# A macaron block on one core: the MLP norm's variance by a ones matmul with its power on ScalarE and GpSimd, inputs shifted by DMA, merged weights kept in DRAM, and a new order of steps

## The chip, the cores and the metric

The kernel runs on one core of a Trainium2 chip. The metric is the device time of one execution in microseconds (us); a lower one is better. Everything is computed in fp32 except a mask product in bf16.

## The reference

The input x has 2048 tokens of 128 features. Three parts follow one another, each added to x: half of a transformer, a state-space block (a scan over time with 16 states per channel), and half of the same transformer with the same weights again. Each transformer first takes a layer norm of x and then runs six layers, each with 16 heads of 64, a window of 32 tokens and an MLP of inner width 341:

```python
for i in range(DEPTH):                      # 6
    x = attn_layer(shift_tokens(x), Wqkv[i], q_scale[i], k_scale[i], Wo[i]) + x
    x = ffn_layer(shift_tokens(x), ln_g[i], ln_b[i], W1[i], b1[i], W2[i], b2[i]) + x

def attn_layer(x, Wqkv, qs, ksc, Wo):
    ...
    q = l2norm(q) * qs                      # t / max(norm(t), 1e-12)
    k = l2norm(k) * ksc
    q = q * cos * scale + rotate_half(q) * sin * scale
    k = k * cos * inv + rotate_half(k) * sin * inv
    return local_attention(q, k, v) ... @ Wo    # each token sees its window and the one before

def ffn_layer(x, g, bln, W1, b1, W2, b2):
    mu = x.mean(-1, keepdims=True)
    var = ((x - mu) ** 2).mean(-1, keepdims=True)
    xn = (x - mu) / jnp.sqrt(var + 1e-05) * g + bln
    a, gate = jnp.split(xn @ W1 + b1, 2, -1)
    return a * jax.nn.gelu(gate, approximate=False) @ W2 + b2
```

`shift_tokens` takes the upper 64 features from the token before.

## The kernel before, in words

Activations stay in SBUF with features on partitions: `r0` feeds the attention, `r1` the MLP, each 2048 columns and a pad of 32; the writers store the upper 64 features one column further on, which is the token shift (`halves`). A tile is 128 tokens, 16 to a layer and 96 to a transformer; a block is four tiles (512 tokens). The attention works on tiles, the MLP on blocks.

The engines run in the order in which `run` issues (a manual schedule for PE, DVE, ACT and POOL; SP, which issues the loads, is left to the framework). `run` goes through iterations i; in each it goes down the list `ORDER` of pairs (step, lag) and issues the step for tile i - lag, so that up to eight tiles are under way. An MLP step runs only for the last tile of a block, in every fourth iteration. A layer's loads, biases and merge are issued at fixed iterations ahead of the list.

The steps of a tile, by the tables `TILE` and `BLOCK`: PQ and PK project queries and keys into PSUM (L252, `x_ps`); SQ and SK square them on ACT (L264); T1 and T2 multiply by cosines and sines on DVE (L270, L276); AQ and AK add the two on POOL (L285); UQ and UK sum the squares on DVE (L291, `ss`). The norm of queries and keys takes a floor at 1e-24 on DVE (NM, `floors`, L298), exp(-0.5 ln) on ACT (NL, `roots`, L303 and L304) and a Newton step of three small DVE products (NN, `norms`, L309, L310, L312). CQ and CK multiply by it on POOL (L316). RQ and RK transpose on PE (L329, `t_ps`), EQ and EK copy out on ACT (L338, L343), EP copies the previous window's keys (L350). S makes the scores: two masks in bf16 (L366) and 64 small products (L377, `s_ps`). MX takes maxima on DVE (L393), ES copies out on ACT (L388), SB subtracts on POOL (L399), EX exponentiates on ACT (L405), SM sums and inverts on DVE (L410, L411), DV divides on POOL (L415), TP transposes on DVE (L425).

The values aren't projected: XT transposes the inputs of the tile on PE, once for its own 128 tokens and once for those 32 earlier (`inputs`, L434, `i_ps`), EXW copies both out in one go (`inputs_out`, L441, `xw`), and PX averages inputs by the attention weights (L450, `z_ps`, 16 instructions on 32-row groups). EZ0 and EZ1 copy that out (L462, `zt`), ZM mixes with 16 matrices of 128x128 that are Wv times Wo per head (L470, `y_ps`), and RS adds the residual (L480). These merged matrices `w.m` are made by `merge` from Wv and Wo, for each layer in each transformer (PE L201, copies on ACT L208).

The steps of a block: F1 centres by a matmul (L492), XC and SF copy and square on ACT (L503, L508). V sums the squares of each token by four matmuls against a column of 1/128 (L88, `v_ps`), so that the variances lie on partitions; VE adds the epsilon on DVE (L518); PW raises to the power -0.5 on POOL and puts it on a diagonal (L108, L110); RB spreads it over partitions by a matmul of ones (L120, `rb_ps`); XN multiplies centred values, gain and spread on DVE (L533). G and A are the two halves of the first MLP product (L543), GL the gelu on ACT with a table load before and after (L562, L670), H the product (L574), Y the second product (L587) and YR the residual (L598).

Large PSUM tiles (`bank2`, two banks) rotate over three buffers, small ones (`bank`) over two. So a product waits until the third `bank2` before it has been read.

## Time and profile before

| | |
|---|---|
| median of 3 runs | 3683.08 us (3682.62 to 3688.38) |
| the profiled execution: its time, its span | 3705.84 us, 3704.0 us |
| granted TensorE clock, mean | 0.957 |
| busy share of the span: PE, DVE, POOL, ACT | 94%, 88%, 71%, 59% |
| mixing products of tiles, first and last: first transformer | 103.6 and 1597.1 us from the start |
| the same, second transformer | 2173.5 and 3668.5 us |
| DMA | 66.50 MB, 18 GB/s on average |

The span is the time from the first to the last instruction in the trace; the run's own time is 1.84 us longer. Busy shares are averages over the two transformers and the state-space block between them (about 1626 to 2095 us), in which DVE works and PE partly waits. A row of a timeline or of the chain of waits gives the start, the duration, the engine, the line, what is written from what and how many instructions are merged. A matmul's duration reaches past the start of the next one, since they are pipelined; the difference of two starts is the time that one took in a full queue. In rows of groups the numbers after the bar are the busy time in us, the mean of one in ns and the idle time ahead of them with what ended it. fp32 products count as two instructions each, transposes as one.

### The profile page before, as it was taken

The page shows a single profiled execution, that of the slowest core. Times are in us where ns is not written, and L with a number is a line of the kernel's source. Part 1 is how long each engine was busy: PE and PEld are TensorE (multiplying, and loading weights), DVE is VectorE, ACT ScalarE, POOL GpSimd, SP SyncE. Part 2 cuts the span into 40 slices and gives each one's busy share as a digit, 9 for nine tenths or more (in the row PEclk, how much of TensorE's full clock was granted, in tenths as well). Part 3 has the DMA queues.
Part 4 walks back from the last instruction along what each step waited for, and adds up shares of the span by engine and source line. Part 5 has one row for each costly group of instructions (what it writes and reads, how often), then busy time and mean ns, then how long its engine had stood idle before and what let it go on. Part 6 is the DMA issues. An engine that isn't in the chain of part 4 may idle for free.

```text
span 3704.0 us, 94599 instructions
## 1 busy us (share of the span) xinstructions
PE 3494.9 (94%) x41968; PEld 2239.0 (60%) x41968; DVE 3259.9 (88%) x3954; ACT 2168.4 (59%) x2884; POOL 2621.3 (71%) x1450
## 2 busy tenths in 40 slices
PE   6999999999999999976999789999999999999997
PEld 3666666666666666642222356666666666666664
DVE  4989999999999999847889778999999999999994
ACT  2666666666666666634222277666666666666664
POOL 4878878888888888721100188888888888888883
PEclk7999999999999999986779899999999999999998
DMA  2000010000000000000000200000001000000000
GB/s 92 13 19 25 13 36 11 26 19 19 19 19 19 8 13 7 2 7 0 1 0 0 68 7 25 19 19 19 25 13 36 8 19 30 13 13 7 14 2 13
DMA packets 45504, 66.50 MB, mean 18 GB/s; under 512 B 2412, under 2 KB 35496, under 8 KB 43560
## 3 DMA queue, kind: packets, MB, share of 16 engines
q1 hardware_dynamic: 45096, 60.45, 5.3%
q8 instruction: 331, 5.42, 0.6%
q14 instruction: 77, 0.63, 0.1%
HBM read 59.39 MB, written 1.05 MB: 16 GB/s over the span
## 4 chain that ended last, share of the span: by engine, by line
PE 27%; DVE 19%; issue 5%; ACT 4%; POOL 1%; DMA 0%; POOLq 0%; DVEq 0%; ACTq 0%
PE y_ps L470 5%; PE x_ps L252 5%; DVE rot L270 3%; DVE ss L291 3%; PE z_ps L450 3%; DVE st L843 2%; PE t_ps L329 2%; PE y L850 2%; PE s_ps L377 2%; DVE t L276 2%; PE a_ps L543 2%; DVE ss L298 2%; PE o_ps L587 2%; DVE rs L410 1%; DVE mx L393 1%
## 5 line engine op out<-in xcount | busy, mean ns | idle before, releaser
L285 POOL TENSOR_TENSOR rot<-rot,t 128x1024 f32<-128x1024 f32 x384 | 900.0, 2364 | 89.2 <-DVE rot L270 86.1
L316 POOL TENSOR_TENSOR rot<-rot,rn 128x1024 f32<-128x1024 f32 x384 | 722.5, 1902 | 135.4 <-DVE rn L312 135.4
L470 PEld LDWEIGHTS y_ps<-zt,m 128*128 128x128 f32 x6144 | 717.5, 192 | 99.6 <-issue 81.9
L470 PE MATMUL y_ps<-zt,m 128*128 128x128 f32 x6144 | 719.0, 275 | 6.3 <-ACT zt L462 6.3
L252 PE MATMUL x_ps<-qk,r 128*128 128x512 f32 x1536 | 703.6, 600 | 10.5 <-ACT zt L462 8.5
L264 ACT ACTIVATE sq<-x_ps 128x1024 f32<-128x1024 f32 x384 | 389.1, 1025 | 447.0 <-DVE t L276 446.3
L415 POOL TENSOR_TENSOR pr<-pr,rs 128x1024 f32<-128x1024 f32 x192 | 364.9, 1900 | 254.9 <-DVE rs L411 253.6
L276 DVE TENSOR_TENSOR t<-x_ps,tab 128x1024 f32<-128x1024 f32 x384 | 461.6, 1203 | 66.1 <-PE x_ps L252 65.7
L252 PEld LDWEIGHTS x_ps<-qk,r 128*128 128x128 f32 x1536 | 285.7, 191 | 356.2 <-issue 313.2
L270 DVE TENSOR_TENSOR rot<-x_ps,tab 128x1024 f32<-128x1024 f32 x384 | 467.3, 1218 | 37.1 <-ACT sq L264 31.3
L291 DVE TENSOR_REDUCE ss<-sq 128x16 f32<-128x1024 f32 x384 | 448.8, 1210 | 1.4
L329 PE MATMUL t_ps<-cs,rot 128*128 128x128 f32 x3072 | 388.7, 278 | 47.0 <-POOL rot L316 46.9
L450 PE MATMUL z_ps<-pt,xw 32*128 32x512 f32 x3072 | 387.9, 614 | 17.0 <-DVE rot L270 13.0
L462 ACT COPY zt<-z_ps 128x1024 f32<-128x1024 f32 x384 | 388.6, 1013 | 25.3 <-PE z_ps L450 21.9
L329 PEld LDWEIGHTS t_ps<-cs,rot 128*128 128x128 f32 x3072 | 352.8, 144 | 80.6 <-POOL rot L316 57.1
L343 ACT COPY kt<-t_ps 128x1024 f32<-128x1024 f32 x192 | 194.6, 1014 | 320.9 <-PE t_ps L329 320.9
L399 POOL TENSOR_TENSOR pr<-pr,mx 128x1024 f32<-128x1024 f32 x192 | 365.3, 1903 | 1.2 <-ACT pr L388 1.2
L377 PEld LDWEIGHTS s_ps<-kt,qt 64*32 64x32 f32 x24576 | 255.3, 105 | 115.7 <-issue 60.7
L377 PE MATMUL s_ps<-kt,qt 64*32 64x64 f32 x24576 | 290.1, 225 | 11.6 <-issue 9.0
L388 ACT COPY pr<-s_ps 128x1024 f32<-128x1024 f32 x192 | 194.5, 1013 | 170.3 <-DVE mx L393 170.3
L298 DVE SCALAR_TENSOR_TENSOR ss<-ss 128x32 f32<-128x32 f32 x192 | 258.1, 1344 | 6.5
L837 ACT ACTIVATE da<-delta,a_neg 128x512 f32<-128x512 f32 x128 | 92.2, 722 | 252.2 <-DVE st L843 247.5
(133 smaller groups left out, 4980.0 us busy)
## 6 DMA issues: line engine op xcount, KB each, us to landing
tab<-in_tabs_dram SPq DMA_DIRECT2D x48, 512.0 KB, 3.5
qk<-in_wqk_dram SPq DMA_DIRECT2D x12, 1024.0 KB, 5.4
wv<-in_wv_dram SPq DMA_DIRECT2D x12, 512.0 KB, 4.2
wo<-in_wo_dram SPq DMA_DIRECT2D x12, 512.0 KB
w<-in_w_dram SPq DMA_DIRECT2D x12, 341.0 KB, 7.4
w<-in_w_dram SPq DMA_DIRECT2D x12, 128.0 KB, 2.1
xi<-in_x_dram SPq DMA_DIRECT2D x4, 256.0 KB
out_dram<-xo SPq DMA_DIRECT2D x4, 256.0 KB
```

The costliest lines, as they stand in the source:

```text
L252: nc.tensor.matmul(out=x[:, j], lhsT=self.r0[:, bass.ds(PAD + g % NT * P, P)], rhs=self.w[g // NT].qk[:, bass.ds(kind * INNER + j * 512, 5 ...
L264: self.nc.scalar.activation(st.sq[kind], st.x[kind], AF.Square)
L270: self.nc.vector.tensor_tensor(st.rot[kind], st.x[kind], cos, ALU.mult)
L276: self.nc.vector.tensor_tensor(st.t2[kind].rearrange("p h (two c) -> p h two c", two=2), st.x[kind].rearrange("p h (two c) -> p h two c", ...
L285: self.nc.gpsimd.tensor_tensor(st.rot[kind], st.rot[kind], st.t2[kind], ALU.add)
L291: self.nc.vector.tensor_reduce(st.ss[:, kind, :], st.sq[kind], AX.X, ALU.add)
L316: self.nc.gpsimd.tensor_tensor(st.rot[kind], st.rot[kind], st.rn[:, kind, :].unsqueeze(2).to_broadcast([P, HEADS, DH]), ALU.mult,)
L329: self.nc.tensor.transpose(t_ps[:, c, :], flat[:, bass.ts(c, P)], self.k.ident)
L377: nc.tensor.matmul(out=st.s[32 * b : 32 * b + 32, par, c, :], lhsT=st.qt[rows, c, bass.ts(b, WIN)], rhs=st.kt[rows, c, bass.ds(WIN * b, 2 ...
L450: self.nc.tensor.matmul(out=st.z[b // 2][:, b % 2].rearrange("p (h q) -> p h q", q=WIN), lhsT=st.xw[rows, j, :], rhs=st.pt[rows, :, j, :], ...
L462: self.nc.scalar.copy(st.zt[:, 2 * half : 2 * half + 2].rearrange("p b h q -> p b (h q)"), st.z[half])
L470: self.nc.tensor.matmul(out=st.y_ps.rearrange("p (b q) -> p b q", q=WIN), lhsT=self.w[g // NT].m[:, h // 2, h % 2, :], rhs=st.zt[:, :, h, ...
```

## The change

In the MLP norm V is one matmul of a 128x128 matrix of ones with the squares, which gives the sum of each token on all partitions. VE (three ACT instructions of 128x512) makes variance plus epsilon and exp(-0.5 ln) of it; XN (five POOL instructions of 128x512) does a Newton step and multiplies by the centred values. PW and RB are gone. The gain goes into W1, which ACT scales once per layer after `biases` has read it. In the norm of queries and keys the floor is a Relu of (ss - 1e-24) on ACT with 1e-24 added again later, and the first of the three DVE products is a Square on ACT. XT transposes the tile's own 128 tokens only; EXW copies them and two DMAs that ACT issues build the half that lies 32 tokens earlier, from this tile (96 partitions) and the one before (32 partitions), with three buffers. In the first transformer SP stores each layer's merged matrices to DRAM after `merge`; in the second it loads them instead of Wv and Wo, and nothing is merged. `ORDER` is new: RQ, RK, EQ, EK, EP, S and MX go from lag 1 to 2, SB, EX and SM from 2 to 3, XT and EXW from 1 to 3, PX, EZ0 and EZ1 from 3 to 4, ZM, RS and F1 from 4 to 5, XN from 5 to 6, A from 6 to 7, UQ and NL from 0 to 1, AQ from 0 to 1; PK stands first among PE's steps of an iteration, PQ stands between PX and S.

```diff
-    ("DV", 3), ("ES", 2), ("XC", 5), ("G", 6), ("NN", 1), ("PK", 0), ("SF", 5), ("CQ", 1),
-    ("GL", 6), ("H", 7), ("PQ", 0), ("CK", 1), ("T2K", 0), ("SK", 0), ("TP", 3), ("T2Q", 0),
-    ("ZM", 4), ("T1K", 0), ("SB", 2), ("Y", 7), ("SQ", 0), ("RK", 1), ("V", 5), ("EK", 1),
-    ("RS", 4), ("T1Q", 0), ("YR", 7), ("VE", 5), ("RQ", 1), ("EQ", 1), ("EP", 1), ("UK", 0),
-    ("PW", 5), ("XT", 1), ("PX", 3), ("RB", 5), ("UQ", 0), ("S", 1), ("F1", 4), ("AK", 0),
-    ("NM", 0), ("EX", 2), ("EZ0", 3), ("AQ", 0), ("XN", 5), ("NL", 0), ("EXW", 1), ("TB", 7),
-    ("EZ1", 3), ("A", 6), ("SM", 2), ("MX", 1),
+    ("SB", 3), ("GL", 7), ("PK", 0), ("AQ", 1), ("T1K", 0), ("SK", 0), ("ZM", 5), ("UQ", 1),
+    ("RS", 5), ("T2K", 0), ("A", 7), ("EX", 3), ("XN", 6), ("RK", 2), ("H", 7), ("RQ", 2),
+    ("EK", 2), ("SM", 3), ("UK", 0), ("EQ", 2), ("NL", 1), ("F1", 5), ("XT", 3), ("NN", 1),
+    ("PX", 4), ("PQ", 0), ("AK", 0), ("EP", 2), ("DV", 3), ("EZ0", 4), ("CQ", 1), ("CK", 1),
+    ("XC", 5), ("S", 2), ("EXW", 3), ("SF", 5), ("EZ1", 4), ("T2Q", 0), ("V", 5), ("ES", 2),
+    ("TB", 3), ("T1Q", 0), ("G", 6), ("Y", 7), ("SQ", 0), ("MX", 2), ("VE", 5), ("TP", 3),
+    ("YR", 7),
...
+        if self.again:
+            w.m = wp.tile([P, 8, 2, P], F32, tag="m", name="m")
+            nc.sync.dma_start(out=w.m.rearrange("p c j f -> p (c j f)"), in_=k.merged[layer])
+            return
...
     def merge(self, layer):
+        if self.again:
+            return
...
+        nc.sync.dma_start(
+            out=self.k.merged[layer], in_=w.m.rearrange("p c j f -> p (c j f)")
+        )
     def biases(self, layer):
...
+        nc.scalar.activation(w.w1, w.w1, AF.Identity, scale=self.vec(V_G + layer))
...
-    def floors(self, g):
-        s = self.at[g].ss
-        self.nc.vector.scalar_tensor_tensor(s, s, 1e-24, s, ALU.max, ALU.max)
     def roots(self, g):
-        st = self.at[g]
+        nc, k, st = self.nc, self.k, self.at[g]
+        nc.scalar.activation(st.ss, st.ss, AF.Relu, bias=k.minus_tiny)
         st.y = self.sb.tile([P, 2, HEADS], F32, tag="y0", name="y0")
-        self.nc.scalar.activation(st.y, st.ss, AF.Ln)
-        self.nc.scalar.activation(st.y, st.y, AF.Exp, scale=-0.5)
+        nc.scalar.activation(st.y, st.ss, AF.Ln, bias=k.tiny)
+        nc.scalar.activation(st.y, st.y, AF.Exp, scale=-0.5)
+        st.y2 = self.sb.tile([P, 2, HEADS], F32, tag="y2", name="y2")
+        nc.scalar.activation(st.y2, st.y, AF.Square, scale=float(np.sqrt(0.5)))
     def norms(self, g):
...
-        nc.vector.scalar_tensor_tensor(y2, st.y, -0.5, st.y, ALU.mult, ALU.mult)
-        nc.vector.scalar_tensor_tensor(y2, y2, 1.0, st.ss, ALU.mult, ALU.mult)
+        nc.vector.scalar_tensor_tensor(st.y2, st.ss, 1e-24, st.y2, ALU.add, ALU.mult)
...
-        nc.vector.scalar_tensor_tensor(st.rn, y2, 1.5, st.y, ALU.add, ALU.mult)
+        nc.vector.scalar_tensor_tensor(st.rn, st.y2, 1.5, st.y, ALU.subtract, ALU.mult)
     def inputs(self, g):
-        st.i_ps = self.bank("i_ps")[:, 0:256].rearrange("p (j f) -> p j f", f=P)
-        for j in range(2):
-            self.nc.tensor.transpose(
-                st.i_ps[:, j, :], self.r0[:, bass.ds(g % NT * P + WIN * j, P)], self.k.ident
-            )
+        st.i_ps = self.bank("i_ps")[:, 0:P]
+        self.nc.tensor.transpose(
+            st.i_ps, self.r0[:, bass.ds(PAD + g % NT * P, P)], self.k.ident
+        )
     def inputs_out(self, g):
-        self.nc.scalar.copy(st.xw, st.i_ps)
+        st.xw = self.sb.tile([P, 2, P], F32, tag="xw", name="xw", bufs=3)
+        nc.scalar.copy(st.xw[:, 1], st.i_ps)
+        nc.scalar.dma_start(out=st.xw[WIN:, 0], in_=st.xw[0 : P - WIN, 1])
+        if g % NT:
+            nc.scalar.dma_start(out=st.xw[0:WIN, 0], in_=self.at[g - 1].xw[P - WIN :, 1])
+        else:
+            nc.gpsimd.memset(st.xw[0:WIN, 0], 0.0)
     def variance(self, f):
-        variances(self.k, ff.sq, ff.v_ps)
+        self.nc.tensor.matmul(out=ff.v_ps, lhsT=self.k.ones, rhs=ff.sq, start=True, stop=True)
     def variance_out(self, f):
-        self.nc.vector.tensor_scalar(ff.ve, ff.v_ps[:, 0:4], LN_EPS, None, ALU.add)
-    def deviation(self, f):
...
-    def spread(self, f):
...
+        ff.ve = sb.tile([P, 512], F32, tag="ve2", name="ve", bufs=1)
+        nc.scalar.activation(ff.ve, ff.v_ps, AF.Identity, bias=k.eps, scale=1.0 / P)
+        ff.rs = sb.tile([P, 512], F32, tag="fsq", name="rs", bufs=1)
+        nc.scalar.activation(ff.rs, ff.ve, AF.Ln)
+        nc.scalar.activation(ff.rs, ff.rs, AF.Exp, scale=-0.5)
     def normal(self, f):
-        nc.vector.scalar_tensor_tensor(
-            ff.xn, ff.xc, self.vec(V_G + layer), ff.rb, ALU.mult, ALU.mult
-        )
+        nc.gpsimd.tensor_tensor(t, ff.rs, ff.rs, ALU.mult)
+        nc.gpsimd.tensor_tensor(t, t, ff.ve, ALU.mult)
+        nc.gpsimd.tensor_scalar(t, t, -0.5, 1.5, ALU.mult, ALU.add)
+        nc.gpsimd.tensor_tensor(t, t, ff.rs, ALU.mult)
+        nc.gpsimd.tensor_tensor(t, ff.xc, t, ALU.mult)
...
-    transformer(k, xt)
+    transformer(k, xt, False)
     state_space(k, xt)
-    transformer(k, xt)
+    transformer(k, xt, True)
```

## The prediction

> **What bounds the kernel now.** I read the busy shares first, then the spacing of one operation over whole layers, then the order of TensorE's work inside one tile. The busy shares:
>
> ```profile
> PE 3494.9 (94%) x41968; PEld 2239.0 (60%) x41968; DVE 3259.9 (88%) x3954; ACT 2168.4 (59%) x2884; POOL 2621.3 (71%) x1450
> ```
>
> Two stretches of about four tiles in the middle of a transformer, from the table by stretches (length, then busy PE, PEld, DVE, ACT, POOL, the clock, the DMA share):
>
> ```profile
> 800.00:863.10 63.10, 62.26 (x849) 42.40 (x848) 58.90 (x74) 40.57 (x54) 52.72 (x29) 1.00 0.03 10
> 863.10:927.00 63.90, 63.51 (x852) 42.99 (x851) 60.66 (x73) 41.16 (x56) 53.99 (x28) 1.00 0.06 18
> ```
>
> PE is busy 125.8 of 127.0 us at full clock, DVE 119.6, POOL 106.7, ACT 81.7. Busy PE can hide stalls, so I take start-to-start times. In the chain of waits the mixing product (L470) of tiles 16 apart, in the second transformer:
>
> ```profile
> 2203.60 3.57 PE y_ps L470 x32
> ...
> 2457.96 3.57 PE y_ps L470 x32
> ```
>
> A layer is 254.4 us (the next two spacings are 254.5 and 254.4). Now the timeline of PE, with a block's norm in the first tile and none in the second:
>
> ```profile
> 866.16 3.73 PE L470 MATMUL y_ps<-zt,m 128*128 128x128 f32 x32
> 869.73 1.04 PE L329 MATMUL t_ps<-cs,rot 128*128 128x128 f32 x8
> 870.60 0.95 PE L88 MATMUL v_ps<-inv,sq 128*128 128x1 f32 x8
> 871.41 1.07 PE L329 MATMUL t_ps<-cs,rot 128*128 128x128 f32 x8
> 872.33 0.38 PE L434 MATMUL i_ps<-cs,r 128*128 128x128 f32 x2
> 872.64 2.00 PE L450 MATMUL z_ps<-pt,xw 32*128 32x512 f32 x16
> 874.57 1.13 PE L120 MATMUL rb_ps<-dg,ones 128*128 128x512 f32 x2
> 875.62 0.39 PE L366 MATMUL s_ps<-masks 32*128 32x512 bf16 x2
> 875.94 1.48 PE L377 MATMUL s_ps<-kt,qt 64*32 64x64 f32 x128
> 877.35 2.84 PE L543 MATMUL g_ps<-xn,w 128*128 128x512 f32 x6
> 880.03 3.60 PE L252 MATMUL x_ps<-qk,r 128*128 128x512 f32 x8
> ...
> 889.27 2.00 PE L450 MATMUL z_ps<-pt,xw 32*128 32x512 f32 x16
> 891.06 0.42 PE L366 MATMUL s_ps<-masks 32*128 32x512 bf16 x2
> 891.41 1.48 PE L377 MATMUL s_ps<-kt,qt 64*32 64x64 f32 x128
> ```
>
> Differences of starts give the price of each group: x 3.43, y 3.57, t 1.74, i 0.45 (0.31 to 0.49), z 1.79, masks 0.35, s 1.41: 12.74 a tile, 203.8 in sixteen. A block adds c 0.97, v 0.86 (0.81, and 0.05 because it splits t), rb 1.16 (872.64 to 875.94 is 3.30; without rb 889.27 to 891.41 is 2.14), g 2.68, a 2.68, o 2.58: 10.93, 43.7 in four blocks. The merge is 2.2 (733.56 to 735.84 in its timeline), the biases 1.4 (17.3 us over 12 layers in the groups). Together 251.1 of 254.4: PE's own work bounds the kernel, with 3.3 us of stall in a layer, 40 in all.
>
> **What the Trainium skill says.** "SBUF — State Buffer", section "SBUF: two separate sides": a VectorE instruction with two SBUF inputs and a GpSimd instruction take a shared port pair exclusively; the later one waits for the whole instruction. The trace agrees: the tiny product L298 takes 1.34 us on average, 0.23 in one tile and 1.78 in another, while L310, of the same shape, takes 0.20. "GPSIMD Engine Reference", section 3.1: a two-input fp32 operation costs GpSimd 1.96 times VectorE's time; here 2.36 us (L285) against 1.20 (L276), 1.97 times. "TensorE: Matmul & The Clock Gate", section "The mechanism" of Part 3: weights load ahead of running matmuls only if row groups differ; the 0.30 us that rb costs above its own 0.86 (two matmuls at x's 0.43) agrees with a lost overlap at a change between row-tiled and full-array work, but shows the price only. "DMA: Bandwidth & Descriptors", section "Anatomy of one DMA": a fixed time of some 2 us, mostly completion; this trace's smallest loads land in 2.1 us.
>
> **The change on PE, the path that sets the end.** (1) One input transpose less a tile: t gives 1.74/16 = 0.11 each; bounds 0.11 to 0.22, taken 0.11, 1.8 a layer. (2) v and rb go, 4 x (0.86 + 1.16) = 8.1; one ones matmul of 128x512 comes, 4 x 0.86 = 3.4. (3) The new order splits x: keys' half ahead of the mixing, queries' half between z and the masks. That puts a full-array matmul between row-tiled ones in every tile: 16 x 0.30 = 4.8 a layer. Bounds 0 (another wait covers the reloading) and 0.45 (half as much again); taken 0.30, since rb stood in the very same place. Sum: 1.6 less a layer, 19 in 12 layers. (4) The second transformer doesn't merge: 6 x 2.2 = 13.
>
> **Off PE, per four tiles of 63.5 us.** DVE loses the floors (L298), one of three steps of the norm, the normalizing product and the epsilon, with these groups of 800 to 1200 us:
>
> ```profile
> L298 DVE SCALAR_TENSOR_TENSOR ss<-ss 128x32 f32<-128x32 f32 x25 | 35.4, 1414 | 0.9
> L309 DVE SCALAR_TENSOR_TENSOR y<-y 128x32 f32<-128x32 f32 x26 | 27.3, 1051 | 0.0
> L415 POOL TENSOR_TENSOR pr<-pr,rs 128x1024 f32<-128x1024 f32 x26 | 49.4, 1901 | 30.7 <-DVE rs L411 30.7
> ```
>
> 4 x 1.41 + 4 x 0.19 + 0.74 + 0.15 = 7.3 of 59.8. The port wait of L309 (1.05 against 0.19) I leave on the new first product, which also has two SBUF inputs; bounds 0.19 and 1.41. DVE isn't the bound, so this is worth only what of PE's 40 us of stall comes from it. POOL loses the power and the diagonal, 1.02 + 1.04, and gains five operations of 128x512. The diagonal at 1.04 and its like at 1024 columns, 1.90, give 0.18 fixed; a product of full operands is then 0.18 + (2.36 - 0.18)/2 = 1.27, four 5.1; the one-input step is bounded by 0.6 (half) and 1.27, taken 0.8: 5.9 together. POOL goes from 53.4 to 57.2. ACT gains two 128x32 activations a tile (0.23 each), three of 128x512 a block (0.63) and two DMA issues a tile, 0.33 to 0.58 in SP's timeline, taken 0.4; the copy falls from 0.35 to about 0.24: 40.9 becomes 47.5. What hides it all is PE's 62. Were the cover gone, each would cost its full size. The issue waits on ACT for the copy ahead of it; behind it queue a block's squares (SF), the second copy of z (EZ1), the scores' copy (ES) and the squares of q (SQ), and PE waits for EZ1 with its next keys' projection. The shifted half lands some 2 to 3 us after issue and is read one iteration later, over 8 us on. POOL's XN, 5.9 in one go, stands ahead of AK, DV, CQ and CK; PE wants the keys' turn 5.3 us into the next iteration (x half 1.7, y 3.6), which is what POOL may be late.
>
> SP is passed too: in the first transformer a store of 1 MB follows each merge and waits on SP for ACT's copies (1.0 each), with the next loads of Wo and of a table behind it, both used iterations later; in the second one load of 1 MB replaces two of 0.5. At a DMA share of 0.03 to 0.06 nothing waits for these. Scaling W1 on ACT (12 times some 0.8) comes several iterations before its use.
>
> The stalls: PE's weight loads for the scores wait 40.1 us in the whole run for ACT (pr L405) and those of x 30.2 (zt L462), ACT in turn for DVE; with longer lags and 7.3 us less DVE half of the 40 should go, bounds none and all: -20. The ends: the last block's chain has nothing beside it. v at the cold clock takes 2.1 instead of 1.05; three ACT steps (1.9) and POOL's 5.9 replace 0.16, 1.01, 1.04, rb 2.07 and xn 0.75: 9.9 against 6.1, +4 an end, +7 for both.
>
> Sum: -19 - 13 - 20 + 7 = -45. It is made against the profiled execution (span 3704.0, run 3705.84), which lies 0.6% over the median of 3683.08; I take the difference off the median: 3638.
>
> **Rivals.** *A, the forecast*: 3638, own range 3612 to 3665. *B, reloading hidden, stalls gone*: the 4.8 a layer falls away and all 40 us go: -58 - 20 more, 3560; half of that, 3600, is likelier. For: the turns of queries and keys and the averaging each stand one iteration later behind their inputs, which leaves slack. Against: rb paid the price in that place. *C, new waits eat the gain*: PE's stalls grow by 3.3 a layer instead of halving, +60 on A, say 3680: for it speak ACT's longer queue ahead of EZ1 and the burst on POOL. *D, slower: POOL's queue becomes the bound.* Its idle time is 10.1 of 63.5 in four tiles, about half of it ahead of L415, waiting for DVE's divisors. POOL's work will be 57.2; if all its waits stay, its cycle is 67.3, 3.8 over today, x 48 blocks = +182: 3865. It decides from 6.3 of the 10.1 us on. Against: DVE, whom it waits for, gets lighter, and the divisors stand early in the new order.
>
> **Numbers.** A 0.50, B 0.22, C 0.15, D 0.13. The measurement can't tell less than 0.2%, 7.4 us, from no change. Faster: A, B and half of C, 0.79; same 0.08 from C; slower D, 0.13. The range is 3575 to 3692: below it lies the end of B, 0.05, above it D, 0.13.
>
> **What would show it.** The 16-tile spacing of y should be near 251 in the first transformer and 249 in the second; z to masks should take 2.2 more than 1.79 (x half 1.72, switch 0.30 and its share); L298 gone, the first product of the norm still near 1 us; the five POOL steps near 5.9. If z to masks shows no price, B holds. If POOL is busy over 95% in the middle and PE waits for POOL's rot, D. If PE waits for ACT zt, C.

## The result and the profile after

| | before | after |
|---|---|---|
| median | 3689.49 us (20 runs, 3677.99 to 3712.70) | 3686.01 us (20 runs, 3664.97 to 3698.81) |
| ratio to before, 95% interval | | 0.9979 (0.9962 to 0.9996) |
| span of the profiled execution | 3704.0 us | 3693.0 us |

The forecast was 3638 from 3683, 45 us less. Measured are 0.2% less, 7.7 us with an interval of 1 to 14 (the two medians lie 3.5 apart): the sign is right, five sixths of the gain are missing. The busy times on the page of the kernel after:

```profile
PE 3483.3 (94%) x41200; PEld 2167.3 (59%) x41200; DVE 3020.2 (82%) x3477; ACT 2338.7 (63%) x3414; POOL 2784.8 (75%) x1606
```

DVE has lost 240 us and PE 12; ACT and POOL have gained 170 and 164. None of that says where the time went, so I cut both spans at the same landmarks, the starts of the mixing products `y_ps` and of the projections `x_ps`. The third column is the first experiment, explained below.

| stage, us | before | after | after, one table load more |
|---|---|---|---|
| start to first mixing product | 103.6 | 102.1 | 105.9 |
| first transformer, first to last mixing product | 1493.5 | 1479.2 | 1478.5 |
| from there, through the state-space block, to the second transformer's first projection | 517.7 | 524.6 | 515.3 |
| first projection to first mixing product | 58.7 | 68.1 | 60.6 |
| second transformer, first to last mixing product | 1495.0 | 1480.0 | 1462.2 |
| last mixing product to end | 35.6 | 39.1 | 38.7 |

The stage with the state-space block takes 491 to 527 us over the fourteen profiled executions, and its length follows the clock granted to PE there: 491 to 494 us at a mean of 0.83 to 0.84 in six of them, 509 to 527 at 0.76 to 0.79 in the other eight. Between the kernel with two transposes below (492.0) and the kernel after (524.6) PE's busy time in this stage is 395 and 437 us, while DVE is busy for 392 and 394 and ACT for 152 in both. That fits the spread of 14 to 47 us between the runs of one kernel, which goes with their mean granted clock, but only one execution of each kernel was profiled. It is why I read stages beside totals.

Two things stand out. The first transformer gains 14.3 us where 20 were forecast. The second gains 15 where 33 were, and loses 9.4 on the way to its first mixing product. Where in the second? Its mixing products 16 tiles apart, from the chain of waits of the kernel after:

```profile
2174.14 3.57 PE y_ps L485 x32
...
2434.67 3.59 PE y_ps L485 x32
...
2685.67 3.59 PE y_ps L485 x32
```

The first sixteen take 260.5, the next 251.0 (before: 250.8 and 254.2). So its layers do run faster, and the loss sits at its head. In the middle (layers two to five of each transformer, y to y) a layer falls from 254.5 to 253.3 in the first transformer and from 254.4 to 250.7 in the second; the prediction expected near 251 and 249. The middle, in the timeline of PE, with a block's norm in the first tile:

```profile
847.15 1.02 PE L507 MATMUL c_ps<-r,cs 128*128 128x512 f32 x2
848.01 0.27 PE L442 MATMUL i_ps<-cs,r 128*128 128x128 f32 x1
848.21 2.00 PE L465 MATMUL z_ps<-pt,xw 32*128 32x512 f32 x16
850.14 1.98 PE L263 MATMUL x_ps<-qk,r 128*128 128x512 f32 x4
852.06 0.39 PE L376 MATMUL s_ps<-masks 32*128 32x512 bf16 x2
852.38 1.56 PE L387 MATMUL s_ps<-kt,qt 64*32 64x64 f32 x128
853.87 1.12 PE L529 MATMUL v_ps<-sq,ones 128*128 128x512 f32 x2
854.83 1.90 PE L263 MATMUL x_ps<-qk,r 128*128 128x512 f32 x4
856.57 3.73 PE L485 MATMUL y_ps<-zt,m 128*128 128x128 f32 x32
...
866.43 1.55 PE L387 MATMUL s_ps<-kt,qt 64*32 64x64 f32 x128
868.09 2.81 PE L556 MATMUL g_ps<-xn,w 128*128 128x512 f32 x6
```

Read it by differences of starts. The variance is one group of 0.96 in place of v and rb (0.81 and 1.06 on average). The queries' half between z and the masks takes 1.92, the keys' half further down 1.74; z takes 1.93 where it took 1.79: the price of changing over that step (3) foresaw. And the scores, 1.41 before, take 1.49 ahead of v and 1.66 ahead of g. That last number is a wait; whose, the second experiment tells. The groups of 800 to 1200 us, busy time and mean ns after the bar:

```profile
L322 DVE SCALAR_TENSOR_TENSOR rn<-y,y 128x32 f32<-128x32 f32 x26 | 26.5, 1018 | 0.9
L320 DVE SCALAR_TENSOR_TENSOR y<-ss,y 128x32 f32<-128x32 f32 x26 | 15.3, 588 | 1.4 <-ACT y L316 1.4
L548 POOL TENSOR_TENSOR xn<-xc,xn 128x512 f32<-128x512 f32 x7 | 9.2, 1311 | 0.5
L545 POOL TENSOR_TENSOR xn<-xn,ve 128x512 f32<-128x512 f32 x7 | 8.9, 1274 | 0.6
...
L544 POOL TENSOR_TENSOR xn<-rs 128x512 f32<-128x512 f32 x6 | 6.3, 1046 | 0.0
...
L546 POOL TENSOR_SCALAR xn<-xn 128x512 f32<-128x512 f32 x7 | 4.3, 619 | 0.6
```

POOL's five steps, L544 to L548, sum to 5.5 (5.9 forecast). The floor L298 is gone, but the last product of the norm, L322, with operands of the same kinds and sizes, took 0.19 before as L312:

```profile
L312 DVE SCALAR_TENSOR_TENSOR rn<-y,y 128x32 f32<-128x32 f32 x26 | 5.0, 192 | 0.9
```

Now it takes 1.02. The wait for POOL that the prediction described for L298 has moved on to it: between 180 and 1540 us 48 of its 86 instructions are long (1.8 us in the median), and each of these began while a POOL instruction ran and ended with it (0.05 us later in the median); the other 38 take 0.19. No run here tests the wait by itself.

### The profile page after: what moved, and what is told of

Its sections match the earlier page's. It is cut to its first block, busy times and chain, and to the rows that moved or that the text cites. A ratio compares the mean times of both kernels' runs of the same rounds, so it can differ in the third digit from the quotient of the medians.

```text
span 3693.0 us, 93340 instructions
## 1 busy us (share of the span) xinstructions
PE 3483.3 (94%) x41200; PEld 2167.3 (59%) x41200; DVE 3020.2 (82%) x3477; ACT 2338.7 (63%) x3414; POOL 2784.8 (75%) x1606
## 4 chain that ended last, share of the span: by engine, by line
PE 78%; DVE 10%; issue 5%; ACT 4%; POOL 2%; ACTq 1%; DMA 0%; POOLq 0%; SPq 0%; DVEq 0%
PE x_ps L263 18%; PE y_ps L485 17%; PE z_ps L465 10%; PE s_ps L387 7%; PE t_ps L339 4%; PE g_ps L556 4%; PE a_ps L556 3%; PE o_ps L600 3%; DVE t L287 3%; PE y L863 3%; DVE st L856 2%; PE s_ps L376 2%; PE c_ps L845 1%; DVE r L495 1%; PE b_ps L845 1%
## 5 line engine op out<-in xcount | busy, mean ns | idle before, releaser
L263 PE MATMUL x_ps<-qk,r 128*128 128x512 f32 x1536 | 758.6, 617 | 10.3 <-ACT sq L275 5.1
L287 DVE TENSOR_TENSOR t<-x_ps,tab 128x1024 f32<-128x1024 f32 x384 | 469.3, 1222 | 82.9 <-PE x_ps L263 73.9
L263 PEld LDWEIGHTS x_ps<-qk,r 128*128 128x128 f32 x1536 | 271.7, 192 | 421.4 <-issue 226.4
L465 PE MATMUL z_ps<-pt,xw 32*128 32x512 f32 x3072 | 400.8, 614 | 13.1 <-DVE t L287 5.2
L339 PE MATMUL t_ps<-cs,rot 128*128 128x128 f32 x3072 | 370.1, 274 | 19.7 <-POOL rot L326 19.7
L425 POOL TENSOR_TENSOR pr<-pr,rs 128x1024 f32<-128x1024 f32 x192 | 365.2, 1902 | 21.3 <-DVE rs L421 13.4
L403 DVE TENSOR_REDUCE mx<-s_ps 128x16 f32<-128x1024 f32 x192 | 235.0, 1224 | 127.1 <-ACT pr L398 125.4
L387 PE MATMUL s_ps<-kt,qt 64*32 64x64 f32 x24576 | 298.5, 227 | 7.0 <-ACT kt L360 7.0
L387 PEld LDWEIGHTS s_ps<-kt,qt 64*32 64x32 f32 x24576 | 267.0, 105 | 55.0 <-issue 45.9
L435 DVE STREAM_TRANSPOSE pt<-pr 128x1024 f32<-128x1024 f32 x192 | 237.4, 1237 | 43.0 <-POOL pr L425 43.0
L850 ACT ACTIVATE da<-delta,a_neg 128x512 f32<-128x512 f32 x128 | 92.2, 722 | 260.3 <-DVE st L856 255.6
```

The source lines that it names most:

```text
L263: nc.tensor.matmul(out=x[:, j], lhsT=self.r0[:, bass.ds(PAD + g % NT * P, P)], rhs=self.w[g // NT].qk[:, bass.ds(kind * INNER + j * 512, 5 ...
L287: self.nc.vector.tensor_tensor(st.t2[kind].rearrange("p h (two c) -> p h two c", two=2), st.x[kind].rearrange("p h (two c) -> p h two c", ...
L339: self.nc.tensor.transpose(t_ps[:, c, :], flat[:, bass.ts(c, P)], self.k.ident)
L387: nc.tensor.matmul(out=st.s[32 * b : 32 * b + 32, par, c, :], lhsT=st.qt[rows, c, bass.ts(b, WIN)], rhs=st.kt[rows, c, bass.ds(WIN * b, 2 ...
L465: self.nc.tensor.matmul(out=st.z[b // 2][:, b % 2].rearrange("p (h q) -> p h q", q=WIN), lhsT=st.xw[rows, j, :], rhs=st.pt[rows, :, j, :], ...
```

## Experiments

My theory after the traces: the middle gains what PE's own sum says, and the queue of ACT, made longer by the change, takes it back in two places: at the second transformer's head, where loads of activation tables (the function tables that ACT needs before a logarithm or an exponential) lie uncovered, and behind the two DMA issues of every tile. The rival: the new order itself is at fault, with its switch between z and the masks, and another order would keep the gain. Each ratio below is to the kernel before, measured beside it on the same chip; the medians of two different experiments were not taken side by side.

### The table loads at the second transformer's head

In the kernel after ACT loads tables twice in each of nine tiles there. Its timeline, with its DMA issues (ACTq):

```profile
2164.61 0.34 ACT L311 ACTIVATE ss<-ss,minus_tiny 128x32 f32<-128x32 f32 x1
2164.97 1.28 ACT L313 ACT_TABLE_LOAD   x1
2166.26 0.32 ACT L313 ACTIVATE y<-ss,tiny 128x32 f32<-128x32 f32 x1
2166.60 1.28 ACT L314 ACT_TABLE_LOAD   x1
2167.89 0.23 ACT L314 ACTIVATE y<-y 128x32 f32<-128x32 f32 x1
2168.16 0.23 ACT L316 ACTIVATE y<-y 128x32 f32<-128x32 f32 x1
2168.29 0.49 ACT L360 ACTIVATE kt<-kt,cs 128x256 f32<-128x256 f32 x1
2168.69 0.99 ACT L477 COPY zt<-z_ps 128x1024 f32<-128x1024 f32 x1
```

and PE in the same moment:

```profile
2169.73 0.39 PE L376 MATMUL s_ps<-masks 32*128 32x512 bf16 x2 [1.97 <-ACT zt L477]
```

The logarithm and the exponential each get a table of their own until the first gelu's load at L683 sets the one that holds both; the explicit load at the head of `run` doesn't appear in the trace of this transformer. The Trainium skill, "ScalarE: Activation LUTs", section "Table sets: the hidden batching unit", gives a logarithm followed by an exponential one load, since one set has both; here a tile shows two. "ScalarE activation tables: per-element evaluation and per-set limits", section "Table sets in the compiler and the runtime", says that the compiler places the loads per block of the program, which fits but is not tested here. The kernel before has the same nine pairs (L303 and L304); the kernel after has two loads more, for its first block's norm (L536 and L537). One explicit load, in the first iteration of each transformer:

```diff
                     getattr(self, method)(g, *args)
+                    if i == 0 and name == "SK":
+                        activation_tables(self.nc, EXP_LN)
```

> The changed kernel with the activation table of exp and ln loaded once at the start of the second transformer, so that the two loads per tile in its first nine tiles (and two for its first block) go. Theory 1 (the gain of the middle was given back at the ends, above all here, where ACT's queue has become longer): the first 16 tiles of the second transformer take 249 to 252 us instead of 260.5, the span 9 to 15 us less than the 3693 of the changed kernel. Theory 2 (the new order's price on PE and new stalls in the middle eat the gain): the head isn't the cause, 0 to 4 us.

Measured: 3664.04 (3639.56 to 3678.17), ratio 0.9898 (0.9848 to 0.9948). The first 16 tiles take 243.9 instead of 260.5, the way to the first mixing product 60.6 instead of 68.1. Of the stages in the table above, 17.8 and 7.5 are gone, 25 us together; the stretch to the first mixing product, which lasts 102 to 107 us over all the profiles, takes 3.8 more.

The same line in the kernel before:

> The kernel before with the same single table load, after the first iteration's last step. Theory 1 (the nine reloaded tables cost only where ACT's queue in the second transformer's head is on the path, which the new queue made it): before's own nine pairs lay beside other work, so at most 3 us of the whole are won, 3690 to 3698 beside before's 3698, and first x to first y of the second transformer stays at 57 to 59 us, its first 16 tiles at 248 to 251. Rival (the loads cost their 2.6 us a tile whatever the queue): 20 us faster as in the new kernel.

Measured: 3699.88, ratio 0.9994 (0.9968 to 1.0021); the head falls from 58.7 to 55.5 and the first 16 tiles from 250.8 to 247.9. So the same loads cost the kernel before 6 us by stages, which is less than its ratio can tell, and the kernel after 25. There too they held up a copy that PE waits for, the second of z:

```profile
2171.70 1.98 PE L252 MATMUL x_ps<-qk,r 128*128 128x512 f32 x4 [1.83 <-ACT zt L462]
```

Apart from two of the twenty loads, then, the change didn't add the loads but their place: now they stand ahead of the copies of the previous window's keys and of both halves of z.

### The shifted inputs: one transpose and two DMAs, or two transposes

On top of the table load, the old `inputs` and `inputs_out`, with two buffers for `xw` as before (not all lines are shown):

```diff
...
+        for j in range(2):
+            self.nc.tensor.transpose(
+                st.i_ps[:, j, :], self.r0[:, bass.ds(g % NT * P + WIN * j, P)], self.k.ident
+            )
...
-        nc.scalar.copy(st.xw[:, 1], st.i_ps)
-        nc.scalar.dma_start(out=st.xw[WIN:, 0], in_=st.xw[0 : P - WIN, 1])
...
-            nc.scalar.dma_start(out=st.xw[0:WIN, 0], in_=self.at[g - 1].xw[P - WIN :, 1])
...
+        self.nc.scalar.copy(st.xw, st.i_ps)
```

> The new kernel with the table load, but with the old inputs: two input transposes and one copy of 128x256 instead of one transpose, a copy of 128x128 and two DMAs issued by ACT. Beside the new kernel with the table load (3664 in its own call). The prediction's step (1): PE does 0.11 to 0.16 us more in each of 192 tiles, 21 to 31 us slower. Rival (ACT's two issues, 1.1 us a tile, are what keeps PE's stalls from falling): slower by less than 10 us or faster.

Measured: 3617.85 (3612.74 to 3643.80), ratio 0.9785 (0.9741 to 0.9830): faster, the opposite of what my step (1) says, and the fastest kernel of this study. Layers take 251.7 instead of 253.1 and 248.5 instead of 250.4; the two transformers lose 12.3 and 11.3 us between their first and last mixing products, 24 in all, and the way to the second's first mixing product is 2.2 longer (62.8 against 60.6), so that 22 remain. The profile of this run has the state-space stage at 492.0, 23 us under that of the run with the table load alone; the clock granted there (0.84 against 0.78) explains this part. Runs of one kernel differ by as much, so the ratio may flatter the change. The lowest times of the two kernels differ by 27. I take 22 to 27 as the effect.

Where it comes from shows in ACT's timeline, in the kernel after:

```profile
864.54 0.99 ACT L477 COPY zt<-z_ps 128x1024 f32<-128x1024 f32 x1
865.43 0.27 ACT L451 COPY xw<-i_ps 128x128 f32<-128x128 f32 x1
865.73 0.52 ACTq L452 DMA_DIRECT2D xw<-xw  x1
866.28 0.61 ACTq L454 DMA_DIRECT2D xw<-xw  x1
866.93 1.01 ACT L477 COPY zt<-z_ps 128x1024 f32<-128x1024 f32 x1 [1.24 <-PE x_ps L263]
```

and with two transposes:

```profile
862.33 0.99 ACT L472 COPY zt<-z_ps 128x1024 f32<-128x1024 f32 x1
863.23 0.37 ACT L451 COPY xw<-i_ps 128x256 f32<-128x256 f32 x1
863.49 1.02 ACT L472 COPY zt<-z_ps 128x1024 f32<-128x1024 f32 x1
```

The second copy of z ends at 867.94 in the first: PE has finished its scores by about 867.8 (1.41 after 866.43) and starts g only at 868.09, behind the copy. With two transposes it ends at 864.51, the scores run from 864.23, and g starts 1.41 later, without a wait. (The label "PE x_ps" on the idle 1.24 misleads, as labels can: the two issues fill it.) In the middle of the first transformer the scores' start to the next start is 1.53 on average with the DMAs and 1.42 without, 0.12 in each tile, 1.9 a layer (2.3 in the second transformer); the second transpose costs PE 0.06 (0.28 to 0.34 at L442 and L444), 0.9 a layer.

Is it ACT's time or the DMA? The same two DMAs from SP's queue:

```diff
-        nc.scalar.dma_start(out=st.xw[WIN:, 0], in_=st.xw[0 : P - WIN, 1])
+        nc.sync.dma_start(out=st.xw[WIN:, 0], in_=st.xw[0 : P - WIN, 1])
...
-            nc.scalar.dma_start(out=st.xw[0:WIN, 0], in_=self.at[g - 1].xw[P - WIN :, 1])
+            nc.sync.dma_start(out=st.xw[0:WIN, 0], in_=self.at[g - 1].xw[P - WIN :, 1])
```

> The new kernel with the table load, the two shifting DMAs of a tile issued by SP's queue instead of ACT's. If ACT's issue time (two issues, 0.55 to 0.6 us each and a wait ahead of each) is what delays the squares and copies behind them: the 16-tile spacing of the middle falls as with two transposes, to 251.5 to 252 in the first and 248.5 to 249 in the second transformer, 20 to 25 us less in all than the new kernel with the table load. If it is the DMA itself or the wait for the copy: the spacing stays at 253.1 and 250.5.

Measured: 3639.26 (3621.41 to 3642.06), ratio 0.9826 (0.9791 to 0.9861). The transformers lose 9.3 and 9.4 us between their mixing products, 19 of the 24; a layer takes 252.4 and 249.1, a little over what I expected. The Trainium skill, "DMA: Bandwidth & Descriptors", section "Issuing engines are not separate DMA queues", says that another issuing engine saves no more than the sequencer's time to initiate a DMA; that is all that is saved here, and it is worth 19 us. So most of the cost is ACT's time for the issues, shown; the rest is small, and even with SP the DMAs are not ahead of a second transpose.

And the two transposes alone, without the table load:

> The new kernel without the added table load, with the old inputs (two transposes and one copy). If the two causes are separate (table loads in the head of the second transformer about 25 us, ACT's DMA issues 24 to 27 us in the middle), it lies about 26 us under the new kernel, middle at 251.7 and 248.5 a layer, and its second transformer's first 16 tiles still near 260, near 3659. If the issues are also part of what uncovers the loads in the head, the first 16 tiles fall towards 245 and the whole towards 3640.

Measured: 3663.99 (3633.20 to 3666.60), ratio 0.9895 (0.9850 to 0.9941), 22 below the kernel after by medians; the stages other than the state-space block give 29. Layers again 251.7 and 248.5, the first 16 tiles of the second transformer at 255.6, between my two numbers: the shorter queue covers some of the table loads, 18 us of them stay (13.4 there, 4.8 ahead of it, against the run with both).

### The order, and the switch between z and the masks

Scores ahead of the queries' half, in the kernel after:

```diff
-    ("PX", 4), ("PQ", 0), ("AK", 0), ("EP", 2), ("DV", 3), ("EZ0", 4), ("CQ", 1), ("CK", 1),
-    ("XC", 5), ("S", 2), ("EXW", 3), ("SF", 5), ("EZ1", 4), ("T2Q", 0), ("V", 5), ("ES", 2),
-    ("TB", 3), ("T1Q", 0), ("G", 6), ("Y", 7), ("SQ", 0), ("MX", 2), ("VE", 5), ("TP", 3),
+    ("PX", 4), ("AK", 0), ("EP", 2), ("DV", 3), ("EZ0", 4), ("CQ", 1), ("CK", 1),
+    ("XC", 5), ("S", 2), ("PQ", 0), ("EXW", 3), ("SF", 5), ("EZ1", 4), ("MX", 2), ("T2Q", 0), ("V", 5), ("ES", 2),
+    ("TB", 3), ("T1Q", 0), ("G", 6), ("Y", 7), ("SQ", 0), ("VE", 5), ("TP", 3),
```

> The changed kernel with the scores (S) ahead of the queries' projection (PQ), so that all row-tiled groups of PE stand together again; MX goes ahead of T2Q. Theory 2: the price of the split vanishes, z back to 1.79, x to 1.72 to 1.75 each; 0.39 us a tile, 6.3 a layer, some 60 to 75 us in all, span 3620 to 3635. Rival: the rotation of the PSUM buffers turns it into waits of the same size (the scores need the buffer that EQ reads), span 3670 to 3710. Theory 1 alone expects no more than 10 us either way.

Measured: 3724.81, ratio 1.0072 (1.0048 to 1.0095). In this kernel's timeline of PE:

```profile
875.69 2.02 PE L465 MATMUL z_ps<-pt,xw 32*128 32x512 f32 x16
877.51 0.41 PE L376 MATMUL s_ps<-masks 32*128 32x512 bf16 x2
878.13 1.48 PE L387 MATMUL s_ps<-kt,qt 64*32 64x64 f32 x128 [0.21 <-ACT kt L360]
```

z to masks is 1.82: without the switch z is as cheap as before, and the scores after the masks take their 1.41. But the masks take 0.62, since the scores now wait for ACT's copy of the keys before (L360), and layers are 255 to 258 in the first transformer. The masks are the smaller part of it, 3.8 us a layer. The two halves of the projection lose more, 4.6 a layer although the switch is gone, where PE waits behind them for ACT, as ahead of g:

```profile
879.73 1.86 ACTq L454 DMA_DIRECT2D xw<-xw  x1
881.62 1.01 ACT L477 COPY zt<-z_ps 128x1024 f32<-128x1024 f32 x1 [2.48 <-PE x_ps L263]
882.78 2.81 PE L556 MATMUL g_ps<-xn,w 128*128 128x512 f32 x6 [1.26 <-ACT zt L477]
```

That copy stands behind the DMA issues, of which the second takes 1.86 here. This order was not run with two transposes, which would take just these issues away. So I tried to give ACT what it needs sooner, EP ahead of EQ and the norm's roots after the first copy of z, with the table load:

```diff
-    ("EK", 2), ("SM", 3), ("UK", 0), ("EQ", 2), ("NL", 1), ("F1", 5), ("XT", 3), ("NN", 1),
-    ("PX", 4), ("PQ", 0), ("AK", 0), ("EP", 2), ("DV", 3), ("EZ0", 4), ("CQ", 1), ("CK", 1),
-    ("XC", 5), ("S", 2), ("EXW", 3), ("SF", 5), ("EZ1", 4), ("T2Q", 0), ("V", 5), ("ES", 2),
-    ("TB", 3), ("T1Q", 0), ("G", 6), ("Y", 7), ("SQ", 0), ("MX", 2), ("VE", 5), ("TP", 3),
+    ("EK", 2), ("EP", 2), ("SM", 3), ("UK", 0), ("EQ", 2), ("F1", 5), ("XT", 3), ("PX", 4),
+    ("AK", 0), ("DV", 3), ("EZ0", 4), ("NL", 1), ("NN", 1), ("CQ", 1), ("CK", 1),
+    ("XC", 5), ("S", 2), ("PQ", 0), ("EXW", 3), ("SF", 5), ("EZ1", 4), ("MX", 2), ("ES", 2),
+    ("T2Q", 0), ("V", 5), ("TB", 3), ("T1Q", 0), ("G", 6), ("Y", 7), ("SQ", 0), ("VE", 5), ("TP", 3),
```

> The new kernel with the table load and another order: the masks and scores ahead of the queries' projection as in the run that put them first, but with their inputs made earlier on ACT (the queries' copy EP ahead of EQ, the norm's roots after the first copy of z). Theory 2 (the queries' half between z and the masks costs 0.39 a tile for nothing but its place): without new waits 60 to 75 us less than the new kernel with the table load, near 3595. Rival (the slot between z and the masks is time that ACT needs for the scores' inputs in any order): the waits stay, 3655 to 3720.

Measured: 3798.12, ratio 1.0254 (1.0213 to 1.0294); layers of 264 and 263. The masks are back at 0.34 us, but DVE now waits 336.5 us for the roots (190 times), and the queries' half waits for ACT's copy of z. Last, with two transposes and the table load, the queries' half ahead of the inputs' transposes, so that nothing stands between z and the masks:

```diff
-    ("EK", 2), ("SM", 3), ("UK", 0), ("EQ", 2), ("NL", 1), ("F1", 5), ("XT", 3), ("NN", 1),
-    ("PX", 4), ("PQ", 0), ("AK", 0), ("EP", 2), ("DV", 3), ("EZ0", 4), ("CQ", 1), ("CK", 1),
+    ("EK", 2), ("SM", 3), ("UK", 0), ("EQ", 2), ("NL", 1), ("F1", 5), ("PQ", 0), ("XT", 3), ("NN", 1),
+    ("PX", 4), ("AK", 0), ("EP", 2), ("DV", 3), ("EZ0", 4), ("CQ", 1), ("CK", 1),
```

> The new kernel with the table load and two transposes (3618 in its call, its middle at 251.7 and 248.5 a layer), with the queries' half ahead of the input's transposes, so that no full-array matmul stands between z and the masks, and what ACT makes for the scores keeps as much time. Theory 2 (the price is that of changing between row-tiled and full-array matmuls, 0.39 a tile, 6.3 a layer): spacing 245.5 and 242.5, 70 to 75 us less in all, near 3545. Rival (the queries' half moved up waits for DVE's keys, or z for ACT, instead): spacing unchanged or more, 3600 or over.

Measured: 3831.01, ratio 1.0361 (1.0317 to 1.0404), layers of 270 and 267, 18 over the 251.7 and 248.5. PE and ACT in this kernel's timeline:

```profile
713.35 2.00 PE L460 MATMUL z_ps<-pt,xw 32*128 32x512 f32 x16
...
715.39 1.01 ACT L472 COPY zt<-z_ps 128x1024 f32<-128x1024 f32 x1 [1.77 <-PE z_ps L460]
...
716.45 0.39 PE L376 MATMUL s_ps<-masks 32*128 32x512 bf16 x2 [1.10 <-ACT zt L472]
```

The masks start when the first copy of z has left PSUM. The queries' half, 1.9 us long, had covered just that. It gets rid of a switch worth 0.35 (0.19 of the projections, the rest of z) and buys 1.10 of waiting: t, queries' half, i and z to the masks sum to 5.96 with two transposes and 7.10 here, 18 us more in sixteen tiles, the 18 measured. My theory of a price paid for nothing falls for this order, in which the switch is the cheaper of two costs. Three orders failed, each at a wait for ACT; whether a fourth does better is open, above all the scores ahead of the queries' half together with two transposes.

### Steps and order apart

The new steps in the old order:

```diff
-    ("SB", 3), ("GL", 7), ("PK", 0), ("AQ", 1), ("T1K", 0), ("SK", 0), ("ZM", 5), ("UQ", 1),
...
+    ("DV", 3), ("ES", 2), ("XC", 5), ("G", 6), ("NN", 1), ("PK", 0), ("SF", 5), ("CQ", 1),
...
```

> All new steps, but the old order of steps (without the three steps that are gone). If the steps are worth what PE's sums say: v, rb and their place 1.16 x 48 = 56, the transpose 21, the merges 13: 90 us less than before, less some 7 at the ends: 3600 to 3640 against 3689. If POOL's burst of five operations or the longer ACT queue is a bound in that order: 3680 or more, with PE waiting for POOL or ACT.

Measured: 4007.70, ratio 1.0823 (1.0770 to 1.0875), layers of about 281 and 279. From the list of waits (total us, times, longest us), PE waits in every block:

```profile
PE g_ps L556 <- POOL xn L548: 179.0, 48, 8.0
```

The old steps in the new order:

```diff
-    ("DV", 3), ("ES", 2), ("XC", 5), ("G", 6), ("NN", 1), ("PK", 0), ("SF", 5), ("CQ", 1),
...
+    ("SB", 3), ("GL", 7), ("PK", 0), ("AQ", 1), ("T1K", 0), ("SK", 0), ("ZM", 5), ("UQ", 1),
+    ("RS", 5), ("T2K", 0), ("RB", 6), ("A", 7), ("EX", 3), ("XN", 6), ("RK", 2), ("H", 7), ("RQ", 2),
+    ("EK", 2), ("SM", 3), ("UK", 0), ("EQ", 2), ("NM", 1), ("NL", 1), ("F1", 5), ("XT", 3), ("NN", 1),
...
+    ("TB", 3), ("T1Q", 0), ("G", 6), ("Y", 7), ("SQ", 0), ("MX", 2), ("VE", 5), ("PW", 5), ("TP", 3),
```

> The old steps in the new order (floors ahead of NL, power and diagonal after the epsilon, the spread after ZM). Theory 2 (the split of x costs PE 0.39 a tile, of which the spread's old place paid a quarter): +60 less up to 40 of removed stalls, 3710 to 3750 against 3689 before. If the order is worth something by itself: 3690 or less.

Measured: 3879.61, ratio 1.0480 (1.0434 to 1.0526), layers of 269. From its list of waits:

```profile
ACT y L303 <- DVE ss L298: 382.3, 187, 3.8
...
PE s_ps L366 <- ACT zt L462: 140.4, 140, 3.2
```

ACT waits 2 us in each tile for the floor on DVE, and behind it in ACT's queue stand the copies that the masks wait for. To see whether the old norm of queries and keys does it, that norm alone (its floor, three products on DVE and no Square on ACT), in the kernel after with the table load:

```diff
-    ("EK", 2), ("SM", 3), ("UK", 0), ("EQ", 2), ("NL", 1), ("F1", 5), ("XT", 3), ("NN", 1),
+    ("EK", 2), ("SM", 3), ("UK", 0), ("EQ", 2), ("NM", 1), ("NL", 1), ("F1", 5), ("XT", 3), ("NN", 1),
...
+        self.nc.vector.scalar_tensor_tensor(s, s, 1e-24, s, ALU.max, ALU.max)
...
-        nc.scalar.activation(st.ss, st.ss, AF.Relu, bias=k.minus_tiny)
...
-        nc.scalar.activation(st.y2, st.y, AF.Square, scale=float(np.sqrt(0.5)))
```

> The new kernel with the table load and the old norm of queries and keys: the floor as a product on DVE with two SBUF inputs (NM ahead of NL), three products instead of two, no relu and square on ACT. The old steps in the new order were 190 us slower, with ACT waiting 382 us for that floor. Theory (the new order needs the floor off DVE, and that is the part of the change that makes it possible): slower by 120 to 190 us, near 3820, ACT waiting for DVE's floors again. Rival (another of the old steps, the ones column and diagonal of the MLP norm or the merge, cost the old steps their time in the new order): slower by less than 60 us.

Measured: 3955.24, ratio 1.0690 (1.0645 to 1.0735), nearly 300 over the kernel with the table load, more than either theory said. Its waits:

```profile
ACT y L316 <- DVE ss L311: 372.8, 188, 3.8
...
PE s_ps L379 <- ACT zt L480: 113.1, 138, 1.3
PE x_ps L263 <- ACT sq L275: 78.4, 46, 2.5
```

The same wait of 2 us per tile as with all the old steps: the new order needs the new norm, and the wait names its floor, though the run put back the whole norm. That it costs more here than with the old steps fits a queue of ACT that also has to issue the DMAs, but I haven't taken that apart.

### POOL's burst

With the table load, and without the Newton step of the MLP norm's power (that part is left out), XN is one POOL operation:

```diff
-        nc.gpsimd.tensor_tensor(t, ff.rs, ff.rs, ALU.mult)
-        nc.gpsimd.tensor_tensor(t, t, ff.ve, ALU.mult)
-        nc.gpsimd.tensor_scalar(t, t, -0.5, 1.5, ALU.mult, ALU.add)
-        nc.gpsimd.tensor_tensor(t, t, ff.rs, ALU.mult)
-        nc.gpsimd.tensor_tensor(t, ff.xc, t, ALU.mult)
+        nc.gpsimd.tensor_tensor(t, ff.xc, ff.rs, ALU.mult)
```

> The new kernel with the table load, without the Newton step of the MLP norm's power on GpSimd: the centred values times ACT's first power, one operation instead of five, so that part of the computation is left out; GpSimd has 4.6 us less in a block. Theory (GpSimd's burst costs only at the two ends): 4 to 5 us less at each end, 8 to 10 in all, the spacing in the middle unchanged at 250 to 253. Rival (the burst is what holds the stalls in the middle as well): spacing 2 or 3 us a layer less, 30 to 45 us in all.

Measured: 3662.34, ratio 0.9885 (0.9843 to 0.9927), no different from the 3664.04 with the step. Layers stay at 253.1 and 250 to 251. At the end the kernel after has

```profile
3671.74 4.26 PE L556 MATMUL g_ps<-xn,w 128*128 128x512 f32 x6 [8.00 <-POOL xn L548]
```

and this one a wait of 3.49 there, 4.5 less; from the last mixing product to the end it takes 34.6 instead of 38.7. The burst of five costs 4 us at an end and nothing in the middle.

## Why the prediction was wrong

Three steps failed: half of the stalls taken as won, the transpose priced on PE alone, and ends at which only the last block's chain was priced. All three put ACT's longer queue at nothing: "What hides it all is PE's 62".

**The bound.** Right: PE is busy 126.2 of 127.0 us in the two stretches that the prediction used, and every gain or loss above is one of PE's own work or of a wait in front of it.

**PE's own sum.** Its total was about right, its terms less so. Starts to next starts per layer, over layers two to five of the first transformer: the two projections and z +5.5 and the masks -0.5, against +4.8 for the switch (taken 0.30, measured 0.35 less 0.03); v for v and rb -3.6, against -4.7; the transposes' group -2.7, against -1.8. Of that last, only 0.9 is the second transpose, by the experiment; the rest came with the new place. With y (-0.4) and c (-0.7) the sum is -2.3 where -1.6 was forecast. The merge was thought to stay as it is in the first transformer; in the new order it takes 3.1 a layer there instead of 2.3, behind ACT's squares. In the second it is gone, and that is worth the 2.3 of before, as forecast (2.2).

The reason that the prediction gave for the switch fits in part. After z the first weights of a projection load 0.002 us ahead of its first product; after o and g they load 0.43 ahead, by the records beside products that still run. So an overlap is lost at the switch, but it isn't lost between two full-array groups, where the row groups don't differ either.

**The stalls, -20: wrong.** This step said that "with longer lags and 7.3 us less DVE half of the 40 should go". Nothing went. The scores' time to the next product grew by 0.3 us a layer in the first transformer and by 1.4 in the second, in place of the 1.65 that was to be won. Two parts of the reasoning failed. DVE's relief was smaller: 240 us in 48 blocks, 5.0 in four tiles, as the port wait went to L322. And the wait that remained wasn't DVE's to give back: it is for ACT's second copy of z, which the prediction had named ("PE waits for EZ1"), with the DMA issues ahead of it at 0.4 each. They measure 0.52 and 0.61, and from the end of ACT's copy to its next instruction 1.2 us pass on average, with two transposes none. With two transposes the scores take 22.6 a layer, 1.41 a tile, which leaves no wait. I had called the issues hidden by PE's 62 us in four tiles. A sum over four tiles doesn't hide a step that stands between two products of one tile.

**Step (1), the transpose: wrong in sign.** It was priced on PE alone, and even there at twice its size: 0.11 a tile, with 0.11 as the lower bound, where the experiment gives 0.06. Taken with the DMAs that replace it, it costs 22 to 27 us in the whole run rather than saving 21.

**The head of the second transformer: not priced.** The prediction asked of the two norms' ends only for the last block's chain. It named ACT's cost "were the cover gone" and didn't ask where the cover is gone: where the pipeline fills, nine pairs of 1.28 us loads, there before too, now stand ahead of PE's next scores. By stages that is 25 us, where the same loads cost the kernel before 6: the difference of 19 is about half of the miss.

**The ends, +7: right where it can be seen, in part by luck.** The tail grew by 3.5, and 4.1 of it go with the Newton step. From v to g it grew by 2.6 (6.5 to 9.1), not by the forecast 3.8, since v took 1.1 there and not 2.1; the rest is a last mixing product longer by 1.6 and other steps that are shorter. At the end of the first transformer the state-space stage's own spread covers it.

The account, after against forecast: first transformer -14 against -20; second -15 against -33, and 9 lost ahead of it; tail +3.5 as forecast. Of the first transformer's -14 the four layers in its middle give 4.9; the rest lies in its first sixteen and last fifteen tiles, for which no run gives a cause. With the head mended the second transformer gives -33, and the whole is 1.0% (0.5 to 1.5) under before, where 1.2% had been forecast. That this meets the forecast is luck in part: the stalls that were to give 10 of it grew, and PE's own sum and the last fifteen tiles gave more than forecast. So the number of case A, not its stalls, describes the change with the table loads gone; case C, "new waits eat the gain", describes what was run, at a place that it didn't name (its own sum, 3638 + 60, is 3698 and not 3680). D didn't come: POOL is busy 57.7 of 63.5 us, as forecast (57.2), and PE doesn't wait for it in the middle. B failed, as the switch has its price in this place.

## What to carry to other kernels

A small cost on an engine "with time to spare" is hidden only if the instructions queued behind it have time to spare: look at what follows it within one tile, and again where the pipeline fills and empties, before calling it free. Replacing work of the bounding engine by DMAs moves their issue into some other queue; price it there, against the next product that waits for that queue. And of an order written out by hand, a step that looks misplaced may be the cover of a copy, so take out steps and order separately before blaming one: here each without the other was 5 to 8% slower than before.

## What the runs showed of the hardware that was not expected

- One operation's price depends on its neighbour: the queries' half takes 1.92 between z and the masks and 1.72 between full-array products, z takes 1.95 ahead of it and 1.82 ahead of the masks with the scores first (medians). The first weights of a projection load 0.002 us ahead of its first product after z, and 0.43 ahead after o or g.
- The wait of VectorE for GpSimd isn't a property of one instruction. With the floor taken away, the next products with two SBUF inputs took it over: 0.59 and 1.02 us at L320 and L322, against 0.19 for the last of them before; each long L322 ended with a POOL instruction.
- The two DMA issues of a tile hold ACT's queue for 0.52 and 0.62 us in the median, in the kernel after; the second took up to 1.69 there, and with the scores first 0.86 in the median and up to 1.86.
- The clock that PE is granted in the state-space block differs from run to run, and that stage's length goes with it: 491 to 494 us at 0.83 to 0.84, 524 to 527 at 0.76.
